# Tokens kept as two partition halves of 56 rows, and the first and last Fourier transform as products of 64 by 64 places

## The chip, the core and the metric

The kernel runs on one core of a Trainium2 chip (trn2). The metric is the device time of one execution in microseconds. Before the change it is 3038.7 us, the median of 3 runs (3035.01 to 3040.98).

## The reference, cut to what matters

Input: 32 images of 56 x 56 places with 96 channels, float32. Three residual layers follow each other, each with a normalization over channels:

```python
# 1: convolution
h  = layernorm(x);  x1 = (h @ w_in + b_in)[..., :192]
x  = x + silu(conv3x3(x1, conv_w) + conv_b)          # 192 -> 96 channels, SAME
# 2: mixing in frequency; the tokens of one image are one sequence of 3136
t  = x.reshape(32, 3136, 96)
h  = relu(bn(layernorm(t) @ w1.T))                   # 96 -> 192
X  = fft(h, axis=1, norm='ortho')                    # over the 3136 tokens
xr = relu(X.real*rd - X.imag*id + rb);  xi = relu(X.imag*rd + X.real*id + ib)
t  = t + bn(ifft(xr + 1j*xi, axis=1).real @ w2.T)    # 192 -> 96
# 3: feed-forward with float8-rounded operands
y  = relu(q(layernorm(t)) @ q(W1).T + b1);  t = t + q(y) @ q(W2).T + b2   # 96 -> 384 -> 96
```

## The kernel before, in words

**Layout.** The tokens of an image stand as 112 partitions x 28 (`N1`, `N2`): a partition holds half an image row, 28 tokens, in seven groups of four (`G4`, `NG`). The Fourier transform over 3136 tokens is split as 112 x 28: a first transform over the 112 partitions (`transform_a`, L241), a transposition through DRAM (`store_a` L464 writes `da`, `fetch_a` L470 reads it back), and a second transform over the 28 tokens with the twiddle factors in its table (`forward`, L256). The way back is the second transform's inverse (`inverse`, L309), a transposition through DRAM (`store_back` L501, `fetch_y` L507), and the last transform (`transform_out`, L317).

**Steps of one image, with the names of the profile.** Convolution: `take_in` (statistics, scaling `xa`, L410), `image` (L165: to channels and the row sums of a Winograd form, `im`, copied to `img` by ScalarE at L167), `make_seam` (L418, L419: the two halves of the picture exchange one column), `conv` (L182 and L186: 24 products `cv` for each of nine parts, each of 32 output channels in one of four column places of the array, so that four go to 32 places each), then sums on VectorE (L195 to L210), SiLU on ScalarE (L211) and transposes back to tokens (`to_tokens`, L219, `st`). Frequency layer: `channels` (L158, `tp_n`), `product_a` (L232, `ph`, then a ScalarE ReLU `h`, L235), `transform_a` (L241, `pa`; ScalarE copies it to `u`, L242), `forward` (L256, `px`; a third of it in two column places of 64), the ReLUs on both engines, `product_w2` (L295, L299, `pg`), `inverse` (L309, `pe`), `transform_out` (L317, `py`), added to the tokens by VectorE (`back_end`, L516). Feed-forward: `ffn_tokens` (L156, `tp_n` in fp8), `ffn_in` (L328, `pf`), `ffn_relu` on VectorE (L335, and the cast to fp8 at L336, `hq`), `ffn_out` (L342, `po`), `ffn_add` (L351, L352).

**Memory.** PSUM has eight banks, two for each of four tags: `a` (`tp_n`, `pf`), `q` (`im`, `cv`, `st`), `b` (`pa`, `pg`, `pe`, `po`) and `c` (`ph`, `px`, `py`). A product waits for a free bank of its tag.

**Order.** Nothing is looped over at run time: the whole program for 32 images is written out. Each step of an image is entered in a list with a due time written by hand, in units of which an image takes eight (`put(when, f, ...)`, in `plan`), so that about three images are in work at once:

```python
            for j2 in range(2):
                put(at + 0.065 + 0.371 * j2, forth, g, j2)
                put(at + 0.536 + 0.659 * j2, forth_a, g, j2)
```

The list is sorted, the steps are emitted, and the tile framework's scheduler then orders instructions on each engine with its own forecast of when each is ready (`schedule_with_timeline_sim=True`). Each engine executes its own list in that order. In `conv` all products but the first of a part are marked `high_priority` and `keep_in_program_order`, so that the scheduler leaves them together.

## Time and profile before

| | |
|---|---|
| median of 3 runs | 3038.7 us |
| span of the profiled execution | 3036.8 us |
| TensorE matmul (PE) busy | 2978.4 us, 98% |
| TensorE weight load (PEld) busy | 2445.3 us, 81% |
| VectorE (DVE) busy | 2348.2 us, 77% |
| ScalarE (ACT) busy | 2277.4 us, 75% |
| GpSimd (POOL) busy | 647.5 us, 21% |
| DMA, all queues | 355.37 MB, mean 117 GB/s |

The profiled execution's span is 3036.8 us; the runs' median is 1.9 us above it, within their spread of 6 us. A row of a group of instructions reads: line, engine, operation, out<-in by the program's names, shapes, number of records, then busy time in us and the mean of one in ns. A product in float32 leaves two matmul records (6912 products of the convolution make 13248 + 576 records), one in fp8 and a transpose leave one. Since matmuls are pipelined, a record's duration is longer than the distance to the next; what a product takes from the engine is read from one start to the next.

### The profile page before, as it was taken

The page shows a single profiled execution, that of the slowest core. Times are in us where ns is not written, and L with a number is a line of the kernel's source. Part 1 is how long each engine was busy: PE and PEld are TensorE (multiplying, and loading weights), DVE is VectorE, ACT ScalarE, POOL GpSimd, SP SyncE. Part 2 cuts the span into 40 slices and gives each one's busy share as a digit, 9 for nine tenths or more (in the row PEclk, how much of TensorE's full clock was granted, in tenths as well). Part 3 has the DMA queues.
Part 4 walks back from the last instruction along what each step waited for, and adds up shares of the span by engine and source line. Part 5 has one row for each costly group of instructions (what it writes and reads, how often), then busy time and mean ns, then how long its engine had stood idle before and what let it go on. Part 6 is the DMA issues. An engine that isn't in the chain of part 4 may idle for free.

```text
span 3036.8 us, 84414 instructions
## 1 busy us (share of the span) xinstructions
PE 2978.4 (98%) x32693; PEld 2445.3 (81%) x32693; DVE 2348.2 (77%) x7248; ACT 2277.4 (75%) x5703; POOL 647.5 (21%) x398
## 2 busy tenths in 40 slices
PE   8999999999999999999999999999999999999997
PEld 7678788888888887888888888888888888888775
DVE  5548777888778887778887778887778887777778
ACT  3467777787777787777787777787777877777877
POOL 2202122222112221122221222221222221121111
PEclk9899999999999999999999999999999999999998
DMA  3533444443454444444444444434444434444443
GB/s 85 144 93 94 117 126 124 118 123 98 121 133 126 117 116 108 122 130 122 123 109 114 125 126 123 127 98 122 124 128 122 123 96 124 129 129 104 113 123 78
DMA packets 495435, 355.37 MB, mean 117 GB/s; under 512 B 329992, under 2 KB 459304, under 8 KB 494808
## 3 DMA queue, kind: packets, MB, share of 16 engines
q1 hardware_dynamic: 493146, 349.24, 43.5%
q8 instruction: 257, 4.21, 0.6%
q10 hardware_dynamic: 1888, 0.74, 0.1%
q14 instruction: 144, 1.18, 0.1%
HBM read 195.73 MB, written 154.14 MB: 115 GB/s over the span
## 4 chain that ended last, share of the span: by engine, by line
PE 88%; DMA 5%; DVE 3%; ACT 2%; issue 1%; POOL 0%; SPq 0%; ACTq 0%; DVEq 0%
PE cv L186 14%; PE ph L232 10%; PE px L256 10%; PE pa L241 9%; PE im L165 7%; PE pe L309 6%; PE pg L299 5%; PE py L317 5%; PE pg L295 5%; PE po L342 4%; PE pf L328 4%; PE cv L182 3%; PE st L219 3%; PE tp_n L158 2%; DMA de<-es 2%; DMA xl<-in_x 1%
## 5 line engine op out<-in xcount | busy, mean ns | idle before, releaser
L186 PE MATMUL cv<-img,wv 97*32 97x196 f32 x13248 | 621.6, 331 | 0.0
L147 POOL TENSOR_TENSOR rs_c<-var_c,mhalf 112x8 f32<-112x8 f32 (+1 forms) x128 | 206.7, 1615 | 1894.1 <-DVE var_c L145 879.1
L186 PEld LDWEIGHTS cv<-img,wv 97*32 97x32 f32 x13248 | 426.8, 109 | 106.9
L235 ACT ACTIVATE h<-ph,rs_b 112x192 f32<-112x192 f32 x896 | 340.1, 449 | 74.1 <-PE ph L232 74.0
L232 PE MATMUL ph<-w1a,n2t 97*112 97x192 f32 x1792 | 381.2, 335 | 2.0 <-ACT n2t L225 0.9
L241 PE MATMUL pa<-h,fa_sb 112*112 112x384 f32 x896 | 372.3, 497 | 0.8 <-ACT h L235 0.8
L330 ACT CAST h<-pf 128x448 f16<-128x448 f32 x672 | 367.5, 567 | 1.1 <-PE pf L328 1.0
L256 PEld LDWEIGHTS px<-fb_sb,at 112*64 112x64 f32 (+1 forms) x3584 | 319.2, 166 | 58.1 <-issue 8.7
L256 PE MATMUL px<-fb_sb,at 112*64 112x112 f32 (+3 forms) x3584 | 353.5, 272 | 8.1 <-DMA at<-da 4.0
L165 PE MATMUL im<-rows_sb,xa 112*97 112x168 f32 x1792 | 321.2, 313 | 2.1 <-DVE xa L410 1.4
L232 PEld LDWEIGHTS ph<-w1a,n2t 97*112 97x112 f32 x1792 | 278.5, 177 | 47.4 <-issue 18.1
L147 POOL TENSOR_TENSOR rs_b<-var_b,mhalf 112x8 f32<-112x8 f32 (+1 forms) x128 | 227.7, 1788 | 397.3 <-DVE var_a L145 310.2
L165 PEld LDWEIGHTS im<-rows_sb,xa 112*97 112x97 f32 x1792 | 264.1, 168 | 33.1 <-issue 15.7
L242 ACT COPY u<-pa 112x384 f32<-112x384 f32 x448 | 226.2, 505 | 75.6 <-PE pa L241 75.4
L272 DVE SCALAR_TENSOR_TENSOR sv<-px,spar_sb,av 128x224 f32<-128x224 f32 (+2 forms) x352 | 152.9, 434 | 151.3 <-ACT av L263 149.8
L336 DVE CAST hq<-h 128x448 fp8e5<-128x448 f16 x672 | 256.1, 386 | 7.5
L335 DVE TENSOR_SCALAR h<-h,b1q 128x448 f16<-128x448 f16 x672 | 220.1, 329 | 40.6 <-ACT h L330 36.1
L299 PE MATMUL pg<-w2x,gt 128*112 128x96 f32 (+1 forms) x1792 | 243.1, 258 | 0.0
L167 ACT COPY img<-im 97x336 f32<-97x336 f32 x448 | 205.5, 461 | 48.6 <-PE im L165 25.8
L299 PEld LDWEIGHTS pg<-w2x,gt 128*112 128x112 f32 (+1 forms) x1792 | 240.8, 178 | 0.0
L261 ACT ACTIVATE av<-px,spar_sb 128x224 f32<-128x224 f32 (+2 forms) x352 | 162.8, 462 | 100.9 <-PE px L256 99.1
L295 PE MATMUL pg<-w2y,gt 128*112 128x192 f32 (+1 forms) x896 | 226.8, 335 | 1.1 <-DVE gt L282 0.7
(121 smaller groups left out, 6197.6 us busy)
## 6 DMA issues: line engine op xcount, KB each, us to landing
da<-u SPq DMA_DIRECT2D x224, 336.0 KB, 3.1
at<-da SPq DMA_DIRECT2D x224, 336.0 KB, 4.2
de<-es SPq DMA_DIRECT2D x448, 84.0 KB, 2.0
y<-de SPq DMA_DIRECT2D x224, 168.0 KB, 2.5
out<-t SPq DMA_DIRECT2D x224, 168.0 KB, 2.6
t<-in_x SPq DMA_DIRECT2D x96, 336.0 KB, 4.4
xl<-in_x SPq DMA_DIRECT2D x93, 336.0 KB, 4.5
t<-in_x SPq DMA_DIRECT2D x32, 168.0 KB, 3.8
```

Source lines behind the costliest of these rows:

```text
L147: nc.gpsimd.tensor_tensor(rs, var, mhalf[:, :n], ALU.pow)
L165: nc.tensor.matmul(ps[:, j], xa[:, j, :], rows6_sb, start=True, stop=True)
L186: tc.keep_in_program_order(nc.tensor.matmul(*args, start=(dx == 0), stop=(dx == 2)))
L232: nc.tensor.matmul(ph[:, j, :], n2t[:, 2 * j2 + j, :], w1a, start=True, stop=True)
L235: nc.scalar.activation(h[:, j], ph[:, j], AF.Relu, scale=rs[:, 2 * j2 + j : 2 * j2 + j + 1])
L241: nc.tensor.matmul(pa, fa_sb, h, start=True, stop=True)
L242: nc.scalar.copy(u[:, 2 * j2 : 2 * j2 + 2, :], pa)
L256: nc.tensor.matmul(px[rows, j], lhs, fb_sb[:, first(p) : first(p + 1)], start=True, stop=True)
L295: nc.tensor.matmul(pg[:, :, j, :], lhs, w2y, start=True, stop=False, skip_group_check=True)
L299: nc.tensor.matmul(pg[:, half, j, :], lhs, w2x, start=False, stop=True, skip_group_check=True)
L330: nc.scalar.copy(h1, pf)
L336: nc.vector.tensor_copy(hq[:, k, :], h2, saturate=False)
```

## The change

- A partition now holds 28 tokens of one half of an image row in another arrangement: 56 rows of 56 tokens, the left 28 in partitions 0 to 55 and the right 28 in partitions 64 to 119 (`HP = 64`, `NQ = 120`). Partitions 56 to 63 are padding; input and output are arranged so on the host (`in_places`).
- The transform is split as 56 x 56. The first and the last transform act on each half alone, 56 places to 56 values: `transform_a` makes four products with 56 rows and 64 columns for each group, one for each of the two partition halves and of the two halves of the output, in 64 x 64 places of the array; both PSUM banks of tag `b` are taken at once. `transform_out` makes four for two groups (two for the seventh), with both banks of tag `c`. Each of these products has 384 columns, as before. The second transform keeps its size.
- `store_a` issues two DMAs for a group instead of one. `fetch_y` reads 56 partitions of 3 KB instead of 112 of 1.5 KB.
- `make_seam` goes; the picture is one piece of 58 columns, and the convolution's columns are picked by an access pattern. The convolution's result rows are written to contiguous places. The row of ones that fed the bias is loaded from a table.
- The feed-forward's cast to fp8 is made once for all three parts of a group, into tiles of 64 places a half with zeros in the pad, and `ffn_out` loads 128 columns of weights instead of 112.
- The order is set anew: `SHIFT` adds to the due times, `back` is entered once for two groups, and the scheduler's forecast is made with shorter queues (`WINDOW`).

```diff
-N1, N2 = 112, 28
-S = 56
-NP = S // 2
+N2, NT1 = 28, 112
+HP = 64
+NQ = HP + HW
+NP = 28
...
+SHIFT = {
+    "back": 0.001, "back_end": -0.054, "conv_end": -0.003, "conv_last": -0.063, "conv_part:2:1": 0.03,
...
+    "tokens_a": -0.021,
+}
...
-    img = const.tile([C + 1, 2, N2 + 2, WC, WG], F32, name="img")
-    ys = [const.tile([113, G4, C], F32, name=f"y{i}") for i in range(4)]
+    img = const.tile([C + 1, HW + 2, WC, WG], F32, name="img")
...
+    ys = [const.tile([NQ + 1, 2, 2, 2, C], F32, name=f"y{i}") for i in range(2)]
+    ss = [const.tile([128, CT, 2, HP], F32, name=f"s{i}") for i in range(2)]
+    hqs = [const.tile([128, 3, G4, 2, HP], F8, name=f"hq{i}") for i in range(2)]
...
+    def together(products, begin=True):
+
+        for i, (to, lhs, rhs) in enumerate(products):
+            if begin and i == 0:
+                nc.tensor.matmul(to, lhs, rhs, start=True, stop=True)
+                continue
+            with tc.high_priority():
+                tc.keep_in_program_order(nc.tensor.matmul(to, lhs, rhs, start=True, stop=True))
+
+    def columns(k, at):
+
+        a = img[:, at : at + CT + N2, k, :]
+        part = tuple(a.ap[0])
+        return bass.AP(a.tensor, a.offset, [part, (WC * WG, CT), (N2 * WC * WG, 2), (1, WG)])
...
-                    cols = img[:, :, CT * t + dx : CT * (t + 1) + dx, k, :]
+                    cols = columns(k, CT * t + dx)
...
-    def transform_a(h, u, b, g, j2):
-
-        pa = psum2.tile([112, 2, H], F32, tag="b", name=f"pa_{b}_{g}_{j2}")
-        nc.tensor.matmul(pa, fa_sb, h, start=True, stop=True)
-        nc.scalar.copy(u[:, 2 * j2 : 2 * j2 + 2, :], pa)
+    def transform_a(h, u, b, g):
+
+        pa = [psum2.tile([128, 2, H], F32, tag="b", name=f"pa_{b}_{g}_{r}") for r in range(2)]
+        together(
+            [
+                (pa[r][HP * c : HP * (c + 1)], fa_sb[HP * r : HP * r + HW], h[HP * r : HP * r + HW, 2 * c : 2 * c + 2])
+                for c in range(2)
+                for r in range(2)
+            ]
+        )
+        for r in range(2):
+            nc.scalar.copy(u[:, r], pa[r])
...
-    def transform_out(y, b, g):
-
-        py = psum2.tile([N1, G4, C], F32, tag="c", name=f"py_{b}_{g}")
-        nc.tensor.matmul(py, ia_sb, y, start=True, stop=True)
+    def transform_out(y, b, q):
+
+        n = min(2, NG - 2 * q)
+        py = [psum2.tile([128, G4, C], F32, tag="c", name=f"py_{b}_{2 * q + r}") for r in range(n)]
+        products = []
+        for h in range(2):
+            for r in range(n):
+                rows = slice(HP * r, HP * r + HW + 1)
+                at = y[rows, :, h].rearrange("p i j c -> p i (j c)")
+                products.append((py[r][HP * h : HP * (h + 1)], ia_sb[rows], at))
+        together(products)
         return py
...
+    def ffn_round(h2, b, g):
+        hq = hqs[(b * NG + g) % len(hqs)]
+        nc.vector.tensor_copy(
+            hq.rearrange("k i j h q -> k (i j h) q")[:, :, :HW], h2.rearrange("k i (t q) -> k (i t) q", q=HW), saturate=False
+        )
+        return hq
...
     def store_a(im, g):
-        nc.sync.dma_start(im.da[g * G4 : (g + 1) * G4].rearrange("n m c -> m n c"), im.u.pop(g))
+        u = im.u.pop(g).rearrange("m r j c -> m (r j) c")
+        for c in range(2):
+            to = im.da[(2 * g + c) * G4 : (2 * g + c + 1) * G4].rearrange("n m c -> m n c")
+            nc.sync.dma_start(to, u[HP * c : HP * c + HW])
...
-    def make_seam(im):
-
-        nc.scalar.copy(img[:, 1, 0], img[:, 0, N2])
-        nc.scalar.copy(img[:, 0, N2 + 1], img[:, 1, 1])
...
         def put(when, f, *args):
+            when += sum(SHIFT.get(key, 0) for key in shifts(f.__name__, args))
             order.append((8 * b + when, len(order), lambda: f(im, *args)))
...
             for j2 in range(2):
                 put(at + 0.065 + 0.371 * j2, forth, g, j2)
-                put(at + 0.536 + 0.659 * j2, forth_a, g, j2)
+            put(at + 0.9, forth_a, g)
...
-            put(at, back, g)
-            put(at + 0.113, back_end, g)
+            if g % 2 == 0:
+                put(at + 0.3, back, g // 2)
+            put(at + (0.45 if g % 2 == 0 else 0.113), back_end, g)
...
+WINDOW = (2, 2, 8)
+
+
+@contextmanager
+def short_window():
+
+    E, depth = mybir.EngineType, TRN2Spec.ENG_ISSUE_QUEUE_DEPTH
+    TRN2Spec.ENG_ISSUE_QUEUE_DEPTH = depth | dict(zip((E.Activation, E.DVE, E.PE), WINDOW))
...
-    with tile.TileContext(nc, schedule_with_timeline_sim=True) as tc:
+    with short_window(), tile.TileContext(nc, schedule_with_timeline_sim=True) as tc:
```

## What the change should do, before it was run

> **What bounds the kernel now.** I read the page first (busy shares, slices, chain), then the groups, then the timeline of single stretches, and last the instruction order of the built program, before and changed.
>
> ```profile
> span 3036.8 us, 84414 instructions
> PE 2978.4 (98%) x32693; PEld 2445.3 (81%) x32693; DVE 2348.2 (77%) x7248; ACT 2277.4 (75%) x5703; POOL 647.5 (21%) x398
> ...
> PE   8999999999999999999999999999999999999997
> ...
> PEclk9899999999999999999999999999999999999998
> ...
> PE 88%; DMA 5%; DVE 3%; ACT 2%; issue 1%; POOL 0%; SPq 0%; ACTq 0%; DVEq 0%
> ```
>
> PE is busy nearly throughout, holds 88% of the chain, and sits idle for 3036.8 - 2978.4 = 58 us in all. Time changes with what PE's own list of instructions takes; VectorE and ScalarE have over 20% to spare. So the question is what each product takes from PE. The rows of the products that change, and of two fp8 weight loads:
>
> ```profile
> L241 PE MATMUL pa<-h,fa_sb 112*112 112x384 f32 x896 | 372.3, 497 | 0.8 <-ACT h L235 0.8
> L317 PE MATMUL py<-y,ia_sb 113*112 113x384 f32 x448 | 192.2, 511 | 14.0 <-DMA y<-de 10.1 <-DVE t L516 1.8 <-issue 1.1
> L342 PEld LDWEIGHTS <-hq 128*112 128x112 fp8e5 x2688 | 180.4, 134 | 55.5 <-issue 20.8 <-DVE hq L336 9.0 <-DVE t L352 1.5
> L328 PEld LDWEIGHTS <-w1q 96*128 96x128 fp8e5 x672 | 66.4, 103 | 16.5 <-issue 2.0
> ```
>
> Means of records overlap, so prices are taken from starts. Two stretches of the timeline (start, length, engine, line, count):
>
> ```profile
> 419.76 0.35 PE L182 MATMUL cv<-img,wv 97*32 97x196 f32 x1
> 419.77 0.37 PE L186 MATMUL cv<-img,wv 97*32 97x196 f32 x3
> 419.95 0.33 PE L182 MATMUL cv<-img,wv 97*32 97x196 f32 x1
> 419.96 2.00 PE L186 MATMUL cv<-img,wv 97*32 97x196 f32 x43
> 421.89 0.91 PE L232 MATMUL ph<-w1a,n2t 97*112 97x192 f32 x4
> 422.63 0.81 PE L241 MATMUL pa<-h,fa_sb 112*112 112x384 f32 x2
> 423.28 0.78 PE L342 MATMUL po<-w2q,hq 128*112 128x96 fp8e5 x12
> ```
>
> ```profile
> 1515.41 0.60 PE L219 MATMUL st<-ident,s 128*112 128x128 f32 x4
> 1515.94 0.35 PE L182 MATMUL cv<-img,wv 97*32 97x196 f32 x1
> ...
> 1518.07 0.32 PE L219 MATMUL st<-ident,s 128*112 128x128 f32 x1
> 1518.22 1.05 PE L256 MATMUL px<-fb_sb,at 112*128 112x114 f32 x8
> ```
>
> The reader is to see three prices. (1) A `pa` product (two records) takes 423.28 - 422.63 = 0.65 us; over all records, start to start, 0.323 each, 0.646 a product; `py`, as wide, the same. (2) Products in different column places run side by side: four of the convolution start within 20 ns, and a round of four takes two passes of 0.163 to 0.166, 0.329 us. A lone one would take as long as four. (3) Changing the form of the places costs. Four `st` take 4 x 0.109 = 0.44 us, but the convolution starts 0.53 after the first. Record by record: from one matmul's modelled end to the next start is -163 ns (median) within one form and -70 ns, nearly without exception, at all 668 changes of form: 93 ns each. The first product in the new form then loses more, because its weights cannot be loaded ahead: 25 ns with 32 columns, 51 with 64, 75 to 91 for the wide float32 ones (`ph`, `pa`, `py`, `pe`), 49 for `st`, 6 for `pf`. The price agrees with `ph` to `pa` above: 0.74 us after the convolution, 0.65 elsewhere.
>
> **The change part by part.** *The meant gain.* `pa`: 448 products x 0.646 = 289 us; if every group's four ran side by side, 224 x 0.646 = 145. `py`: 224 x 0.646 = 145; 128 sets x 0.646 = 83. Saved: 206 us.
>
> *What the order makes of it.* The four are meant to stand together, but the built program separates them. The first pair waits for the first half of `h`, the second for the second half, and each half for a PSUM bank; other steps are placed between, and where a convolution part is also marked to stand together, the scheduler deals out both in turn:
>
> ```
> pa 64x384 (rows 0, cols 0); pa (rows 64, cols 0); ph x2
> cv x14; pa (rows 0, cols 64); cv x1; pa (rows 64, cols 64); cv x9
> ```
>
> Counting the whole list: the 896 `pa` products stand in 93 sets of four, 35 of three, about 68 pairs and 281 alone; the 448 `py` in 60 sets of four and 118 alone. A stretch of one form takes as long as its fullest place, so `pa` has some 478 stretches x 0.646 = 309 us (+19 against before) and `py` 218 x 0.646 = 141 (-4). The convolution, 222 stretches before, is in 581, 179 of them one product long: 1940 rounds for 1729, 211 x 0.329 = +69 us. The 64-column `px` are cut in 1 and 3 in 32 images: 32 x 0.19 = +6.
>
> *Changes of form.* 670 in the list before, 2001 now: 1331 x 0.093 = +124 us. First-product losses: before 222 x 0.027 + 128 x 0.051 + 320 full ones, by kind, 23.5 = 36 us; now 581 x 0.027 + 694 x 0.051 (64 x 64, taken as the 64-column row) + 162 x 0.051 + 564 full ones, many of them `pf` and `po` that lose little, 24 = 83 us: +47.
>
> Here a rule is weighed. The trace shows 93 ns at changes between forms that share the array's columns; it cannot tell whether a product in columns 64 to 127 may start while a convolution product works in columns 0 to 31. The Trainium skill, "TensorEngine Tiling (Array Packing)", Key Properties, says that a change of mode, not of place, empties the array. By the rule no overlap: +69 and +19 stand as above. Without it, starting each product when its own places are free and keeping the 93 ns, the same list comes out 130 us shorter. I take the rule; its other end is in the range. A second rule: no product before uses row places, so nothing in the trace shows that rows 0 to 63 and 64 to 127 work at once. The Trainium skill, "TensorE: Matmul & The Clock Gate", Measured speedup vs the span model, gives 3.07 times for four row places: taken as side by side. If not, the stretches with both row halves take twice as long: counted over the list, +270 us.
>
> *Smaller terms on PE.* `hq` loads 128 columns of fp8 instead of 112. The nearest row is `w1q`, 128 columns in 103 ns against 134 for 112. A `po` record is 52 ns from the next, while 112 columns of `tp_n` in fp8 take 49; freed of its loads, 96 columns would need about 43 (estimate): 2688 x 9 = at most -24 us, at least 0; I take -20, by that row. Transposes to channels stream 120 columns for 112: 896 x 7 ns = +6. Weights of 120 columns (`ph`, `st`): up to 1792 x 8 columns of load, hidden behind passes of 162 ns: 0.
>
> *Off PE.* `make_seam` (L418, L419: 9.0 + 12.5 us of ScalarE), the contiguous result rows (L203, 169 us of VectorE, perhaps a quarter less) and the single cast (L336, 256 us, a little less) shorten engines that are not the bound: 0. What hides a wait for them is PE's list; the cover grows with it. The cast now ends about 0.8 us later for a group (three casts' worth, 1.2 us, after the last ReLU instead of 0.39); `po` stands a median of 8 us of PE work behind the last `pf`, so 0, at worst 0.8 x 224 = 179 if nothing stood between. Two `u` copies of 505 ns (L242) follow a set at once and hold both banks of tag `b`: behind them stand `pg`, `pe`, `po`. Bounds: 0, and one copy for each of 224 + 128 sets, 178 us; the rows of before (PE idle before `pa`, `pg`, `pe` and `po` is 3.5 us in all) say 0. SP issues 224 more stores (347 ns median, +78 us on a queue that spends 690 us of the span on issues) and they land in some 3 us; the reads of `da` follow much later: 0. 7% more bytes for `x` and the output at 44% DMA load: 0.
>
> *Sum.* Stream +19 - 4 + 69 + 6 + 6 - 20 = +76; changes +124 + 47 = +171; together +247. 3036.8 + 247 = 3284, and 1.9 us more for what the median has over this execution's span: **3286 us**, 8% slower.
>
> **The rivals.** *The row halves do not run at once:* 3286 + 270 = 3555. Against it the rule above; for it, no row of this trace.
>
> *Overlap across forms where places are free, each change still at 93 ns:* 3286 - 130 = 3155. For it: every change in the trace is between forms that both fill all columns, so the 93 ns could be a wait for places in use. Against: the rule.
>
> *The other side: to and from 64 x 64 places nothing is emptied or charged.* Then the list's stream, each product starting when its own places are free, is 7 us below before's instead of 90 above; with -14 for the smaller terms and 57 fewer changes among the old forms (x 0.15 = -9): 3009 us, 1% faster. It decides where 1331 added changes cost under about 16 ns each with overlap (21 / 1331); every old kind of change costs 93.
>
> *The change does not do what it says:* if the quartets ran unseparated, the gain of 206 us would stand, with 704 added changes at about 0.144 = +101 and -14: 2920 us. Against it: before, the trace's records follow the built program's list, so the changed list is what PE will execute.
>
> **How the numbers follow.** Main forecast 0.72; partial overlap 3155, 0.10; serial row halves 3555, 0.08; free changes 3009, 0.05; quartets whole 2920, 0.03; an outcome within 0.2% by offsetting terms 0.02. A difference of 0.2% (6 us, the spread of the runs shown) is about what a measurement can tell from none. Faster: 0.05 + 0.03 = 0.08; same 0.02; slower 0.90. The range takes in partial overlap with -15 below it (3140), and upward half of the bank and cast bounds' larger one, some 110 us (3400); serial row halves and the faster cases stay out.
>
> **What the changed profile would show.** PE busy still near 98% with a longer span; `cv` records, now 13,824 as before, with a longer total; in the timeline a lone `pa` of two records 0.65 us long between convolution records, with a step of about 0.1 us at each side; in whole sets four `pa` records starting within some 20 ns. `po` records closer together, and the `hq` load near 103 ns. Wrong would be: `pa` running over convolution records, no step at changes, whole sets that take 1.3 us (serial halves), or PE waiting for ScalarE's `u` and `y` copies by tens of microseconds (a bank wait that I put at 0).

## The result, and the profile after

The changed kernel takes **3391.4 us** (median of 4 runs, 3374.3 to 3411.4) against 3038.4 us for the kernel before on the same chip: ratio 1.1155, 95% interval 1.1108 to 1.1203. It is 11.6% slower, where 8.1% was forecast (3286 us, range 3140 to 3400). The profiled execution took 3374.3 us, its span is 3372.5.

The page after, in the lines that answer to those of before: busy time, PE's slices and clock, and the chain by engine.

```profile
span 3372.5 us, 86673 instructions
PE 3270.6 (97%) x34037; PEld 2351.6 (70%) x34037; DVE 2298.1 (68%) x6800; ACT 2270.6 (67%) x5639; POOL 610.1 (18%) x400
...
PE   8999999999999999999999999999999999999987
...
PEclk9999999999999999999999998999989999999997
...
PE 71%; DVE 14%; DMA 11%; POOL 1%; ACT 1%; issue 1%; SPq 0%; POOLq 0%; ACTq 0%; DVEq 0%
```

PE is still busy 97% of a longer span, so most of the 336 us are work or stretched records on PE. But its share of the chain fell from 88% to 71%: VectorE and the DMAs took 25% where they had 8%. That is the sign of what the forecast left out.

The groups that answer to the rows of before (busy us, mean ns of one, idle before):

```profile
L184 PE MATMUL pa<-h,fa_sb 56*64 56x384 f32 x1344 | 362.6, 511 | 1.9 <-ACT h L258 1.0 <-issue 0.9
L181 PE MATMUL pa<-h,fa_sb 56*64 56x384 f32 x448 | 192.3, 509 | 0.4 <-DVE w1q L876 0.4
L384 PE MATMUL po<-w2q,hq 128*128 128x96 fp8e5 x2688 | 157.5, 210 | 43.9 <-DVE hq L374 43.9
L384 PEld LDWEIGHTS <-hq 128*128 128x128 fp8e5 x2688 | 131.3, 100 | 77.1 <-DVE hq L374 59.4 <-DVE gt L310 8.7 <-issue 1.2
```

`pa` has 1792 records where it had 896. Each is as long as before, since it streams the same 384 columns; only side by side do they gain. The load of `hq` went from 134 to 100 ns. The last column of `po` shows something new: 43.9 us idle for the cast at L374. Before, the same row had 1.2 us in all:

```profile
L342 PE MATMUL po<-w2q,hq 128*112 128x96 fp8e5 x2688 | 184.4, 216 | 1.2 <-DVE hq L336 0.8
```

The timeline shows both outcomes of the four-place form: a whole set of four products, and single ones between convolution records.

```profile
1505.43 0.60 PE L243 MATMUL st<-ident,s 128*120 128x128 f32 x4
1505.97 0.53 PE L181 MATMUL pa<-h,fa_sb 56*64 56x384 f32 x1
1505.97 0.55 PE L184 MATMUL pa<-h,fa_sb 56*64 56x384 f32 x3
1506.34 0.48 PE L181 MATMUL pa<-h,fa_sb 56*64 56x384 f32 x1
1506.35 0.50 PE L184 MATMUL pa<-h,fa_sb 56*64 56x384 f32 x3
1506.78 0.36 PE L364 MATMUL pf<-n3t,w1q 96*128 96x448 fp8e5 x1
...
1517.42 1.32 PE L209 MATMUL cv<-img,wv 97*32 97x196 f32 x23
1518.68 0.85 PE L184 MATMUL pa<-h,fa_sb 56*64 56x384 f32 x2
1519.46 0.52 PE L209 MATMUL cv<-img,wv 97*32 97x196 f32 x2
1519.91 0.85 PE L184 MATMUL pa<-h,fa_sb 56*64 56x384 f32 x2
1520.70 1.18 PE L209 MATMUL cv<-img,wv 97*32 97x196 f32 x18
```

Four products (eight records, in both row halves and both column halves) take 1506.78 - 1505.97 = 0.81 us, the change of form behind them included. One product alone takes 1519.46 - 1518.68 = 0.78 us. A fourth of the work, the same price.

### The profile page after: what moved, and what is told of

Same layout as the page of the kernel before. It is cut to its first block, busy times and chain, and to the rows that moved or that the text cites. A ratio compares the mean times of both kernels' runs of the same rounds, so it can differ in the third digit from the quotient of the medians.

```text
span 3372.5 us, 86673 instructions
## 1 busy us (share of the span) xinstructions
PE 3270.6 (97%) x34037; PEld 2351.6 (70%) x34037; DVE 2298.1 (68%) x6800; ACT 2270.6 (67%) x5639; POOL 610.1 (18%) x400
## 4 chain that ended last, share of the span: by engine, by line
PE 71%; DVE 14%; DMA 11%; POOL 1%; ACT 1%; issue 1%; SPq 0%; POOLq 0%; ACTq 0%; DVEq 0%
PE cv L209 14%; DMA xl<-in_x 9%; PE px L285 7%; PE ph L256 7%; PE pa L184 5%; PE pe L338 5%; PE pg L328 4%; PE pa L181 4%; PE pg L324 4%; PE pf L364 3%; PE po L384 3%; PE cv L205 3%; PE im L170 2%; PE py L181 2%; PE st L243 2%; PE py L184 2%
## 5 line engine op out<-in xcount | busy, mean ns | idle before, releaser
L144 POOL TENSOR_TENSOR rs_c<-var_c,mhalf 120x8 f32<-120x8 f32 (+1 forms) x128 | 197.3, 1542 | 1676.3 <-DVE var_c L142 1666.8
L256 PE MATMUL ph<-w1a,n2t 97*120 97x192 f32 x1792 | 392.8, 339 | 1.8 <-DVE sv L304 1.6
L184 PE MATMUL pa<-h,fa_sb 56*64 56x384 f32 x1344 | 362.6, 511 | 1.9 <-ACT h L258 1.0
L271 ACT COPY u<-pa 128x384 f32<-128x384 f32 x448 | 202.1, 484 | 226.3 <-PE pa L184 225.1
L258 ACT ACTIVATE h<-ph,rs_b 120x192 f32<-120x192 f32 x896 | 329.0, 424 | 27.4 <-PE ph L256 23.4
L256 PEld LDWEIGHTS ph<-w1a,n2t 97*120 97x120 f32 x1792 | 278.2, 184 | 53.7 <-issue 24.8
L170 PE MATMUL im<-rows_sb,xa 120*96 120x168 f32 x1792 | 311.2, 312 | 2.4 <-DVE t L473 0.9
L144 POOL TENSOR_TENSOR rs_a<-var_a,mhalf 120x8 f32<-120x8 f32 (+1 forms) x128 | 215.4, 1692 | 318.6 <-DVE var_a L142 318.5
L170 PEld LDWEIGHTS im<-rows_sb,xa 120*96 120x96 f32 x1792 | 253.9, 164 | 26.9 <-ACT img L175 10.9
L134 DVE BATCH_NORM_STATS2 st_a<-xl 120x6 f32<-120x192 f32 x434 | 131.8, 352 | 188.7 <-DMA xl<-in_x 187.5
L364 PE MATMUL pf<-n3t,w1q 96*128 96x448 fp8e5 x672 | 222.7, 364 | 9.7 <-ACT n3t L359 4.1
```

What stands on the lines that cost most here:

```text
L144: nc.gpsimd.tensor_tensor(rs, var, mhalf[:, :n], ALU.pow)
L170: nc.tensor.matmul(ps[:, j], xa[:, t0 + j, :], rows_sb, start=True, stop=True)
L184: tc.keep_in_program_order(nc.tensor.matmul(to, lhs, rhs, start=True, stop=True))
L256: nc.tensor.matmul(ph[:, j, :], n2t[:, 2 * j2 + j, :], w1a, start=True, stop=True)
L258: nc.scalar.activation(h[:, j], ph[:, j % 2], AF.Relu, scale=rs[:, j : j + 1])
L364: nc.tensor.matmul(pf, w1q[:, k * 128 : (k + 1) * 128], n3t, start=True, stop=True)
```

## How the time is accounted for

For the profiled execution of each kernel I add three things: the **list** (the built order of PE's instructions with the forecast's prices: a stretch of one form lasts as long as its fullest place, each change 93 ns, each first product its loss), the **stalls** (by how much the gaps between PE's records exceed -163 ns within a form and -70 ns at a change) and the **lost clock** ((1 - granted clock) x span). All in us:

| kernel | changes of form | list | stalls | lost clock | sum | span | rest |
|---|---|---|---|---|---|---|---|
| before | 670 | 2888 | 61 | 30 | 2979 | 3036.8 | 58 |
| after | 2001 | 3137 | 116 | 57 | 3310 | 3372.5 | 62 |

The list is a count and not a measurement; what supports it is that the rest, some 60 us, is nearly the same in both. So the added 336 us are: list +249, stalls +55, lost clock +27, rest +4. The sum of the experiments' kernels comes out as well (the rest lies between 33 and 72 us in all those counted below), and so each run can be read in these terms. A median run lost more clock than the profiled one: with 3374, 3386, 3397 and 3411 us the granted clock was 0.983, 0.976, 0.976 and 0.972, and after taking off the lost clock (57, 81, 81 and 95 us) the four are 3317, 3305, 3316 and 3316. The spread of this kernel is mostly its clock.

## The experiments

**1. The sets held whole.** Is it the splitting of the sets that costs? The four products are ordered so that the last one to become ready comes first, and the first product of each set and of each convolution part is put behind the last product of the set or part before it in PE's order (an order, not a wait).

```diff
-                for c in range(2)
-                for r in range(2)
+                for c in (1, 0)
+                for r in (1, 0)
...
-                nc.tensor.matmul(to, lhs, rhs, start=True, stop=True)
+                behind(nc.tensor.matmul(to, lhs, rhs, start=True, stop=True))
...
+    def behind(ins):
+        if block:
+            tc.add_manual_dep(ins.ins, block["last"].ins.name, NoSync)
+        block["last"] = ins
```

> The changed kernel with the sets kept together as far as the scheduler allows: within a set the product that is ready last is put first, and the first product of each set and of each convolution part is issued behind the last product of the set or part traced before it. Nothing is computed otherwise. In the built list there are 1476 changes of form instead of 2001, 99 lone products in 64 x 64 places instead of 399, and the convolution stands in 280 stretches instead of 581; stream, changes and first-product losses counted with the prices of the prediction fall from 3137 to 2858 us, by 279. Theory (the separated sets and the changes of form are the loss): 3391 - 279 = about 3110 us, and down to 3060 if the granted clock returns to 0.99. Rival (the loss lies in the new waits or in the layout, and the sets are a side show): over 3300 us.

Measured: 3404.4 us (3378.9 to 3419.4), ratio 1.1176 (1.1128 to 1.1224): no gain. Yet the list did what it should, 1476 changes and 2858 us, 279 less than after and 30 less than before. The account: list 2858, stalls 277, lost clock (1 - 0.927) x 3417.6 = 249, rest 33. The waits of PE:

```profile
PE py L194 <- DMA y<-de: 106.3, 30, 5.7
PE po L397 <- DVE hq L387: 25.6, 43, 2.4
```

Thirty waits, about one for each of the 32 images, 3.5 us each, for the tokens `y` that come back through DRAM. Between an image's last inverse product `pe` and its first `py` the list of before holds 10.1 us of PE work (median, by the same prices), that of after 13.2, this one only 7.7: the copy `es`, its store, and the load of `y` no longer fit behind it. And the clock, in the stretch ahead of one such wait's end, after it, and then (the column after POOL is the granted clock):

```profile
842.00:850.30 8.30, 4.51 (x43) 3.98 (x41) 8.27 (x25) 5.66 (x15) 4.92 (x4) 1.00 0.89 201
850.30:860.00 9.70, 9.66 (x78) 4.69 (x78) 4.39 (x17) 2.42 (x6) 4.06 (x3) 0.65 0.53 150
860.00:870.00 10.00, 9.84 (x138) 6.71 (x140) 8.14 (x22) 8.87 (x24) 0.09 (x1) 1.00 0.32 88
```

PE stood still for 3.31 us of the first stretch, until 850.34; then 0.65 is granted over 9.7 us, which is half speed for some 7. Of this run's half-speed episodes, all 36 between its first 110 and its last 60 us begin at a pause of PE of over 0.8 us; they last 3.4 to 20.5 us, 10.2 in the median. The Trainium skill, "TensorE: Matmul & The Clock Gate", Part 1, says that an idle window of some 3.4 us halves the clock. The pauses here are of about that length, and all of them together cost about as much again (lost clock 249, stalls 277). That the pause makes the clock drop is the page's statement and fits the order in time; no run here sets the clock by itself. Which pauses are followed by half speed, and which are not, is read from the traces in the last section.

**2. The sets held whole, and the cast by parts.** The single cast at L374 ends later than the three casts of before; is that the cause?

```diff
-        if k == 2:
-            im.hq[g] = ffn_round(im.h2.pop(g), im.b, g)
+        im.hq[g] = ffn_round(im.h2[g], im.b, g, k)
```

> As the kernel with the sets kept together, but the feed-forward's cast to fp8 is made for each of the three parts as soon as it is ready, as before the change, instead of once for all three. PE's list counts 2858 us, like the other's. Theory that the single cast makes PE wait (44 us idle before po in the changed kernel's profile): 40 to 50 us faster than the kernel it is made from, about 3060 us. Rival (PE's list hides the cast, and what is waited for is VectorE's queue as a whole): within 10 us of it, or slower by VectorE's longer list.

Measured: 3411.8 us (3399.6 to 3432.8), ratio 1.1235 (1.1185 to 1.1286). The wait of `po` stays, 23.7 us, and that of `py` too, 108.2. The merging of the casts alone is not the cause.

**3. The changed kernel without its new due times.** The change also brings `SHIFT`, a table that moves steps in the planned order. Here it is empty.

```diff
-SHIFT = {
-    "back": 0.001, "back_end": -0.054, ...
-}
+SHIFT = {}
```

> The changed kernel with all corrections of the due times set to 0 (SHIFT empty), nothing else. The built list has 1905 changes of form, 267 lone products in 64 x 64 places and 419 stretches of the convolution; by the same prices 3039 us, 98 less than the changed kernel. Theory: 3391 - 98 = about 3290 us, if the waits stay as they are. Rival (the new due times were needed to keep PE from waiting): at or above 3391 us, with more PE idle time than 102 us.

Measured: 3413.5 us (3409.5 to 3417.6), ratio 1.1234 (1.1215 to 1.1253), 22 us above after. List 3039, 98 below after; stalls 186, of them 105.1 for `y` in 30 waits; lost clock (1 - 0.964) x 3415.8 = 123; rest 68. So the table buys the absence of the wait for `y` (1.5 us in after), with sets split more often. It also brings the wait of `po`: without the table, and with the same single cast, `po` waits for `hq` 1.7 us in 3 places, in after 43.9 us in 53.

**4. The new layout, without 64 by 64 places.** The tables are made block-diagonal and `pa` and `py` use the whole array again. With them the due times of the two transforms go back to those of before, and `y` to four tiles of one group each, read by two DMAs; layout, single cast and the rest of `SHIFT` stay.

```diff
-    fa_sb = const.tile([NQ, HP], F32, name="fa_sb")
+    fa_sb = const.tile([NQ, 2 * HP], F32, name="fa_sb")
...
-        pa = [psum2.tile([128, 2, H], F32, tag="b", name=f"pa_{b}_{g}_{r}") for r in range(2)]
-        together([...])
+        pa = psum2.tile([128, 2, H], F32, tag="b", name=f"pa_{b}_{g}_{c}")
+        nc.tensor.matmul(pa, fa_sb, h[:, 2 * c : 2 * c + 2], start=True, stop=True)
```

> The changed kernel with its layout (56 rows in two partition halves), its single cast and its corrections of due times, but the first and last transform made with products over the whole array: the 56 x 56 table stands twice on the diagonal of a 120 x 128 one, one product of 384 columns for two tokens columns of both halves, as many products as before the change (448 and 224). 820 changes of form, no 64 x 64 places; 2892 us by the same prices, against 2888 for the kernel before. Theory (the loss is in the 64 x 64 places as they were ordered): 3040 to 3100 us, the upper end if the wait for the single cast stays. Rival (layout, padding or cast cost it): over 3200 us.

Measured: 3211.8 us (3206.8 to 3215.1), ratio 1.0569 (1.0549 to 1.0588). Its list is 2892 us with 820 changes, as good as before's 2888, and still it is 175 us slower than before: stalls 170 (63.9 for `y`, 33.6 more ahead of `px`), lost clock (1 - 0.971) x 3213.3 = 93, rest 58. That is the rival's side. Taking the 64 by 64 places out shortens the list by 245 us and the time by 180; layout, cast and order, without the four-place products, cost some 175 us that the list does not show. Which of the three does, this run does not separate.

**5. Whole sets, and the first last-transform pair due later.** If the wait for `y` is the loss of experiment 1, `back` of the first pair of groups can come three quarters of a planned unit (some 9 us) later.

```diff
-    "tokens_a": -0.021,
+    "tokens_a": -0.021, "back:0": 0.75, "back_end:0": 0.75, "back_end:1": 0.3,
+    "ffn_second:5": 0.12, "ffn_end:5": 0.12,
```

> The kernel with the sets kept together (e1), with three due times moved so that the list of PE holds more work behind which what it waits for can arrive: the first last-transform of an image 0.75 units later (12.6 us of listed work between the last inverse product and it, instead of 7.7), the second feed-forward product of the sixth group 0.12 later; the two column halves of the last transform in the order of the changed kernel. By the same prices the list takes 2857 us, like e1's 2858. Theory (e1 lost its 279 us to 3.3 us waits for y once an image and to the half clock that follows each): the waits go, the granted clock returns to about 0.99, and the time is 2857 + 57 (what all four lists so far took beyond the count) + 60 of waits + 30 of half clock = about 3005 us, 1% under the kernel before. Rival (the half clock comes from the 64 x 64 places themselves, which load the array less): clock stays under 0.95 and the time over 3250 us.

Measured: 3325.3 us (3314.8 to 3328.0), ratio 1.0933 (1.0916 to 1.0950). The wait for `y` fell only from 106.3 to 87.3 us, for a reason of the kernel's own making: with two `y` tiles the load of groups 4 and 5 goes into the tile that the delayed product has yet to read. It reads those later groups in place of its own, and waits for them. The question stayed open, and experiment 9 puts it again. The text's rival, that the half clock comes from the 64 by 64 places, is answered by experiment 4: that kernel has none of them, and its trace has 30 half-speed stretches between its first 110 and its last 60 us, for 3 before.

**6. Before, with `hq` loaded as 128 columns.** One part of the change alone.

```diff
-        po = psum2.tile([N1, G4, C], F32, tag="b", name=f"po_{b}_{g}")
+        po = psum2.tile([128, G4, C], F32, tag="b", name=f"po_{b}_{g}")
...
-                    po[:, j, :], hq[:, k, j * N1 : (j + 1) * N1], w2q[:, k, :],
+                    po[:, j, :], hq[:, k, j * N1 : j * N1 + 128], w2q[:, k, :],
```

> The kernel before, with one part of the change alone: ffn_out loads 128 columns of fp8 weights instead of 112 (the 16 beyond a token column's own are the next one's, and what they give is not read). Theory (112-column fp8 loads bound the distance of po records, 52 ns, and 128-column ones do not, 43 ns): 2688 x 9 ns = 24 us faster, about 3014 us. Rival (hidden, or the longer row of weights costs as much): within 6 us of 3038.

Measured: 3038.0 us against 3040.0, ratio 0.9995 (0.9985 to 1.0005): no difference. The record itself is as forecast, loads of 99 ns for 134 and 43 ns from one `po` to the next for 52, 24 us over 2688. But:

```profile
PE py L318 <- DMA y<-de: 19.2, 22, 2.9
```

The wait for `y`, 10.1 us before, is 19.2 now, and all stalls went from 61 to 75: more than half of the gain on PE came back as stalls that the longer list had covered. The clock fits the remainder: the median over the 14 runs is 0.987, over the 19 of before 0.990, some 9 us more lost.

**7. Before, with the first transform in two column places.** The price of changes of form, in the old kernel and alone.

```diff
-        nc.tensor.matmul(pa, fa_sb, h, start=True, stop=True)
+        nc.tensor.matmul(pa[:64], fa_sb[:, :64], h, start=True, stop=True)
+        with tc.high_priority():
+            tc.keep_in_program_order(nc.tensor.matmul(pa[64:], fa_sb[:, 64:], h, start=True, stop=True))
```

> The kernel before, with the first transform's product split over two column places of 64 (56 columns and 8 of padding each), side by side in one bank; one store more for a group. The array's work is the same as before (448 x 0.646 us); what is added is changes of form: 1502 in the built list for 670. By the prices of the prediction 3010 us for 2888, so +122. Theory: about 3160 us, or up to 30 more if a longer wait brings the half clock. Rival (a change of form costs next to nothing where the next weights are known, and the loss of the changed kernel was in its waits): under 3070 us.

Measured: 3172.9 us (3169.9 to 3174.8), ratio 1.0437 (1.0422 to 1.0452), 133 us more. The list has 1502 changes for 670 and is 122 us longer; stalls 65 for 61, lost clock 41 for 30, which together make 137. The price of a change, with its first-product loss, holds here with no other part of the change present but the second store of a group.

**8. The changed kernel, with `po` of two groups later.** Meant to remove the new wait of `po` for `hq`. In after's trace 52 of its 53 places are at the sixth and the seventh group of an image.

```diff
+    "ffn_second:5": 0.12, "ffn_end:5": 0.12, "ffn_second:6": 0.12, "ffn_end:6": 0.12,
```

> The changed kernel with two due times moved: the second feed-forward product of the sixth and the seventh group 0.12 units later, so that at least 6.5 us of listed work stand between the last first product and it, in place of 3.2 and 4.4. The built list comes out with 1921 changes of form and 3068 us by the same prices (changed kernel: 3137). Theory (po waited for the cast, 53 us in all, and its pauses brought part of the half clock): 3391 - 69 - 50 - 40 = about 3230 us. Rival (the wait moves to the next step in line and the clock does not follow): 3320 us, the list's difference alone.

Measured: 3338.3 us (3333.0 to 3340.2), ratio 1.0980 (1.0966 to 1.0994), 53 us faster than after, but 108 above what was expected. The list also fell, by 69 to 3068. The wait for `hq` is down to 1.6 us, and

```profile
PE px L285 <- DVE t L558: 45.8, 29, 3.3
```

stands in its place: `px` waits for a PSUM bank until VectorE's addition (L558) has read the last `py` out of it. Stalls are 135, for 116 in after, and the lost clock is 57 as in after. So the gain is no more than the list's, and the rival held: the wait moved on and the clock did not follow.

**9. Experiment 5 with three `y` tiles.** Now no later load can reach the tile early.

```diff
-    ys = [const.tile([NQ + 1, 2, 2, 2, C], F32, name=f"y{i}") for i in range(2)]
+    ys = [const.tile([NQ + 1, 2, 2, 2, C], F32, name=f"y{i}") for i in range(3)]
```

> The version with the sets held whole and the first last-transform pair due later, with a third token tile, so that this pair no longer waits for the loading of later groups into its own tile. Its built list has 1518 changes of form and counts 2877 us with the prices of the trace (2137 for the changed kernel as built is not meant here: that one counts 3137). Theory (the whole sets lose their gain to one wait for the tokens of the last transform, once an image, and to the half clock that follows each such pause): the work listed between the last inverse product and the first last-transform product is now 10.4 us a median image against 7.7, so the wait for y falls from 106 to under 40 us, the stalls from 277 to some 120, the lost clock from 252 to some 60: 2877 + 50 + 120 + 60 = about 3105. Rival (the wait only moves on to the next consumer, as it did from po to px in the changed kernel): stalls stay over 220 and the clock below 0.965, 3250 to 3330.

(The list of the kernel that ran counts 2857 us, not 2877, with 12.6 us of work between `pe` and `py`, not 10.4; 2137 is a slip.) Measured: 3347.4 us (3339.7 to 3358.4), ratio 1.1023 (1.0996 to 1.1049). The wait for `y` is 0.7 us in all, as theory had it, and the time did not follow: the rival's side. Waits of PE, and of VectorE:

```profile
PE px L298 <- DVE t L571: 120.9, 31, 5.4
```

```profile
DVE st_a L134 <- DMA xl<-in_x: 197.0, 91, 5.0
```

Thirty-one waits again, 3.9 us each, now at `px`. The chain of waits shows how one arises:

```profile
1644.79 5.94 DMA xl<-in_x
1650.73 0.02 issue
1650.75 0.04 DVE st_a L134
...
1653.17 0.47 DVE t L405
1653.63 0.77 DVE hq L387
1654.41 0.48 DVE t L571
1654.88 0.04 issue
1654.93 1.79 PE px L298 x16
```

A load of the next image's tokens is issued at 1644.79 and lands at 1650.73. The statistics that read it stand at the head of VectorE's order, so all behind them wait: the cast, the addition that frees the bank, and with it `px` on PE. These statistics waited for `xl` 59.0 us in 39 places before (L141 there) and 187.5 us in 87 after (L134).

**10 and 11. The token load due earlier.** In the changed kernel and in version 9: 14 us earlier in the plan, four tiles `xl` instead of three.

```diff
-    "fetch": 0.124,
+    "fetch": -1.0,
...
-            im.xl[i] = xnp.tile([NQ, j1 - j0, C], F32, tag="xl", bufs=3, ...)
+            im.xl[i] = xnp.tile([NQ, j1 - j0, C], F32, tag="xl", bufs=4, ...)
```

> The changed kernel with the second reading of the tokens (xl) issued about 14 us earlier in SP's queue and with four xl tiles instead of three, all else as it was; its built list is the same 2000 changes of form, 3136 us by the prices of the trace. In the changed kernel's chain of waits 9.2% of the span is the load of xl from x (before: not among the lines named), and VectorE waits for it 187.5 us in 87 places against 59.0 in 39. Theory A (that load, standing in SP's queue behind stores that wait, holds VectorE, and behind it hang the cast for po and the copies that PE waits for): the wait falls under 60 us, PE's stalls from 116 to about 60 and with them the mid-run half clock, 3391 to about 3330. Theory B (PE's list sets the time and VectorE's waits lie beside it): the wait falls but the time stays within 15 us of 3391.

> The version with sets held whole, later last transform and three token tiles, with the same earlier xl load and four xl tiles. Its list counts 1520 changes and 2857 us (counted again, the version without the early load has the same list, with 12.6 us of listed work ahead of the first last-transform product; 2877 and 10.4 in its own text came from another build). There the wait for y went from 106 to 0.7 us, but px waited 120.9 us for VectorE's t, which stood behind statistics of xl whose load came late (10.4% of the chain). Theory A: px's wait falls under 40 us, stalls from 289 to about 170, lost clock from 137 to about 80: 2857 + 57 + 170 + 80 = about 3165. Theory B (once an image some consumer waits 3 to 5 us whatever is moved, since the ring through DRAM and the engines' orders sets the length of an image): another wait takes its place and the time stays at 3300 to 3350.

Measured: 3376.1 us (3374.3 to 3393.5), ratio 1.1118 (1.1084 to 1.1151), and 3331.2 us (3327.2 to 3343.0), ratio 1.0970 (1.0939 to 1.1001). The edit hardly did what it says. VectorE still waits 182.0 and 184.6 us for `xl`: the scheduler put most of the loads back to where they had been in SP's order, some 5 to 6 us ahead of their use. In version 11 `px` waits 92.4 us for 120.9, stalls 266 for 289. Theory A was not tried by these two.

**12. The same with the loads held at their place.** As 11, and SP keeps the loads in program order for every image.

```diff
-            in_turn(im.xl[i], im.tokens[:, j0:j1, :], im.b < 3)
+            in_turn(im.xl[i], im.tokens[:, j0:j1, :], True)
```

> As the version with sets held whole, later last transform, three token tiles and four xl tiles, but the loads of xl are held at their place in program order for every image (before, only for the first three images). In the version before this one the scheduler had put them back behind the stores, so its earlier due time changed little: a load was issued a median of 5 to 6 us ahead of the statistics that read it, as in all the versions. Now the built SP queue has them some 10 entries, 20 us or more, further ahead; PE's list is the same (1520 changes, 2857 us). Theory A (the late load holds VectorE, and behind it hangs px): VectorE's wait for xl falls from 184.6 us to under 40, px's wait for t from 92.4 to under 40, stalls from 266 to about 170, lost clock from 130 to about 80: 2857 + 57 + 170 + 80 = about 3165. Theory B (another wait takes the place once more): VectorE's wait falls, the time stays at 3280 to 3350.

Measured: 3403.8 us (3395.9 to 3419.0), ratio 1.1185 (1.1154 to 1.1215): slower than 11, and outside both theories. The list is the same 2857; stalls 285, lost clock (1 - 0.930) x 3417.2 = 239. The wait of `px` is nearly gone, and PE now pauses in the middle of the last transform's set:

```profile
PE py L197 <- issue: 101.1, 27, 5.2
```

"Issue" says that the profile names no releaser. In the timeline (start, length, engine, line) one of these pauses runs from 1599.4 to 1604.6:

```profile
1600.73 3.30 POOL L144 TENSOR_TENSOR rs_a<-var_a,mhalf 120x8 f32<-120x8 f32 x2 [18.88 <-DVE var_a L142]
...
1602.46 0.95 DVE L463 TENSOR_TENSOR xa<-xl,rs_a 120x768 f32<-120x768 f32 x1
1603.34 0.44 DVE L314 SCALAR_TENSOR_TENSOR sv<-px,spar_sb,av 128x224 f32<-128x224 f32 x1
...
1604.06 0.44 DVE L317 SCALAR_TENSOR_TENSOR sv<-px,spar_sb,av 128x224 f32<-128x224 f32 x1
...
1604.60 0.91 PE L197 MATMUL py<-y,ia_sb 57*64 57x384 f32 x3 [5.24 <-issue]
```

`py` and `px` share one tag of PSUM banks. The products go on within 0.1 us of VectorE's last reading of `px` (L317, to 1604.50), and that reading stands behind the scaling `xa`, which waits for GpSimd's power. Only the load of the third chunk became early (9.8 us ahead of its use, median), the others stayed at 3 to 5 us, and VectorE's wait for `xl` was 183.0 us. So the late load was taken away in none of the runs.

**What all of it says.** The kernels with whole sets, in the terms of the account:

| kernel | list | stalls | lost clock | span | rest | the wait that repeats each image |
|---|---|---|---|---|---|---|
| 1 | 2858 | 277 | 249 | 3417.6 | 33 | `py` for `y`, 106 |
| 9 | 2857 | 289 | 137 | 3337.9 | 55 | `px` for VectorE's `t`, 121 |
| 11 | 2857 | 266 | 130 | 3325.4 | 72 | the same, 92 |
| 12 | 2857 | 285 | 239 | 3417.2 | 36 | inside the `py` set, 101 |

The list is 280 us shorter than after's in each, and the stalls lie between 266 and 289 wherever the wait was moved to. A pause of 3 to 4 us an image does not go away by moving the step that shows it. What sets it is not settled. The load of `xl` with VectorE's order behind it is the best supported by the chain of version 9, but no run removed it. Its lead alone does not decide: the four loads of an image are issued a median of 4.0 to 5.5 us ahead of the statistics before, and 3.4 to 6.2 us after.

## Why the prediction was right or wrong

**The main mechanism: right.** *The sets are split, and a lone product costs what four do.* The timeline shows it (0.78 us and 0.81). *A change of form costs 93 ns:* from a modelled end to the next start it is -163 ns within a form and -70 ns at a change (within 5 ns at 1973 of the 2001 in the trace, those to and from 64 by 64 places too); experiment 7 confirms the price in the kernel before. *Row halves work at once:* the whole set shows it, so the rival at 3555 falls. *No overlap across forms:* the convolution records resume only when a lone `pa` is done, so 3155 falls, and with it the free changes at 3009. *The first-product losses* of the new form were 50 ns for 51. *The `hq` load* brings 9 ns a record, as taken. The list's growth was forecast at +247 and counts +249, which is the same built order counted again; its independent support is the unchanged rest and experiment 7. In the time the places weigh less than in the list, since a shorter list uncovers waits: 180 us for 245 in experiment 4.

**What failed: the waits, put at 0.** The step was "so 0, at worst 0.8 x 224 = 179 if nothing stood between", argued from a median of 8 us of PE work behind the last `pf`. In the trace `po` waits in 53 places, 43.9 us in all, and stalls grew by 55 us. The median of 8 us stood for all groups, and two of the seven had much less: 3.2 and 4.4 us of listed work at the sixth and the seventh (the text of experiment 8), where 52 of the 53 waits are. Given at least 6.5 us there, the wait fell to 1.6 us. What used up the cover was VectorE's order, as the chain of waits into one of these pauses shows (start, length):

```profile
2048.51 6.66 DMA xl<-in_x
...
2055.19 0.63 DVE st_a L134 x2
...
2057.68 0.87 DVE xa L450
...
2058.83 0.87 DVE hq L374
...
2059.74 0.68 PE po L384 x12
```

The cast stands behind statistics that wait for a load. Off-PE work was costed at nothing because VectorE and ScalarE have 20% to spare. Free time on an average says nothing of what stands ahead of one cast in that engine's order. The bank wait, put at 0 as well, stayed small in after (stalls of 2 to 4 us each ahead of `pa`, `pg` and `pe`), but a wait for a bank is what came up in experiments 8 and 9. That 3391 lies inside the range is in part luck: its upper end, 3400, allowed some 110 us for waits and nothing for the clock, while the excess of 105 us is about half waits and half clock; the slowest of the four runs, 3411, lies above it.

**What was missing: the clock.** No term of the sum held it. It is +27 us in the profiled execution and some 50 in a median run (81 us lost in the two middle runs, 30 before). Most of it in the profiled run follows from the wait above: of 119 us at half speed (61 before), 44 lie in two stretches, and each begins in or just behind a wait of `po` for the cast. The first wait ends at 2059.74 after 1.29 us, the second at 2478.01 after 2.24 us. The 3.41 us ahead of the first stretch, and the stretch:

```profile
2057.75:2061.16 3.41, 2.12 (x26) 1.25 (x24) 3.37 (x6) 1.78 (x5) 2.29 (x1) 1.00 1.06 229
2061.20:2081.70 20.50, 20.50 (x129) 9.38 (x129) 9.09 (x32) 5.00 (x12) 4.51 (x3) 0.50 0.35 95
```

For 20.5 us PE is busy throughout and its clock is 0.50. A busy share of 97% hides this: 10 of these microseconds were lost. So a wait of 1.29 us was followed by a loss eight times its length, and behind the term that was mis-sized (44 us of `po` for `hq` in place of 0) stand 22 us more of lost clock. They would not have come back with that wait alone: experiment 8 has next to none of it and still loses 57 us, behind other pauses. That a pause makes the clock drop is read from the order in time, not tried by itself.

**The quick rival, "quartets whole, 2920".** It was thought to fail because the sets would not stand whole. Experiment 1 made them stand much more often and its list came to 2858, yet the time was 3404. The rival fails for another reason: in the new layout and order a list of 2857 to 2892 us (experiments 1, 4, 9, 11, 12) no longer covers the waits, with stalls of 170 to 289 us, where before had 61 at 2888. The sum over PE's list, which served for +249, does not serve for -280. Experiment 6 shows the like on a small scale in the old kernel: 24 us less on PE, and none of it in the time.

## What to carry to other kernels

Count a change on the busiest engine from the order in which its instructions will be issued, not from products saved: a product that fills one of four places costs as much as four if other forms stand on both sides of it, and each change of form has its price on top (93 ns, and for the first product 6 to some 95 ns by its kind, here). A sum over one engine's list holds while that list is the cover for everything else; where the list gets shorter, look first for the chains that it covered (here `pe` to store to load to `py`, about 11 us an image), since the gain can stop there. Look at the shortest cover and not at the median, and at what stands ahead in the other engine's order. And put a price on pauses of the tensor engine apart from their length, because the half clock behind them can cost as much again.

## What the runs showed of the hardware that was not expected

- The clock after pauses. In before, after, and versions 1, 9, 11 and 12 every half-speed stretch away from the start and the end has a pause of PE of over 0.8 us in the 3.41 us ahead of it. Not every pause is followed by one: in after 11 of 42 are, and the longest that is not has 2.05 us, while one of 1.29 us stands before a stretch of 20.5. The steps of the clock tell why. In each trace they lie on one grid of 3.41 us, to within 7 ns. The pause of 1.29 us lies in one window of it, in which PE has records for 2.12 us, 0.62 of the window (the row 2057.75 above). The pause of 2.05 us, from 322.95 on, is shared by two:

```profile
320.36:323.78 3.42, 2.59 (x22) 2.35 (x20) 3.35 (x14) 3.23 (x9) 3.19 (x3) 1.00 0.95 191
323.78:327.19 3.41, 2.19 (x32) 1.35 (x34) 3.38 (x9) 0.85 (x3) 1.52 (x1) 1.00 0.89 199
327.19:330.60 3.41, 3.41 (x18) 0.86 (x12) 1.77 (x7) 0.63 (x2) 1.23 (x1) 1.00 0.84 240
```

  PE has records for 0.76 and 0.64 of them, and the clock stays at 1.00. The traces of all 14 kernels hold 12081 windows at full clock between their first 110 and last 60 us. Of 262 with records for less than half, each was followed by half speed; of 11672 with more than 0.64, none; of the 147 between, 70. So it is the busy share of a window that tells, and not the length of a pause; the page cited above asks for an idle window, and here a window with PE busy for half to three fifths of it could be enough. How long half speed then lasts, one to seven windows in after, with PE busy in most of them, no run here explains.
- Four products in both row halves and both column halves, float32, keep the pace of one: the second passes start 0.37 us after the first, of which 50 ns is the loss of the first product, and the other 0.32 is one record's own pace.
- A saving of 24 us on an engine that is busy 98% of the span (experiment 6) was not seen in the time at all (ratio 0.9995, 0.9985 to 1.0005).
